# A four-layer conv and attention hybrid: the first layer's tables of batches two to four, made during batch one

## The chip, the cores and the metric

The kernel runs on one core of one Trainium2 chip. The time is device microseconds of one execution of the whole program; five runs were timed, and one more execution was taken by the hardware profiler.

## The reference, cut to what matters

The input x has 4 batches of 64 x 64 positions and 128 channels, in fp32. Four layers follow each other; each adds its result to x:

```python
x = x + _L0_conv_ref(_gn(x), ...)     # deformable attention over 9 points, 4 groups
x = x + _L1_conv_ref(_gn(x), ...)     # linear attention
t = t + _L2_attn_ref(_ln_t(t), ...);  t = t + _L2_ffn_ref(_ln_t(t), ...)   # 64 experts
t = t + _L3_attn_ref(_ln_t(t), ...);  t = t + _L3_ffn_ref(_ln_t(t), ...)   # spectral filters
```

Layer 0 works on the group-normalised image. A 1x1 product and a 3x3 depthwise convolution give q, k and v. From q come, for each position, 36 offsets (4 groups of 9 points) and a mask. At each offset position k and v are sampled with the four neighbours' bilinear weights; the nine samples of a group are then attended to by q, and the result is projected.

```python
out = gather(y0, x0) * (1 - wy_) * (1 - wx_) + gather(y0, x0 + 1) * (1 - wy_) * wx_ \
    + gather(y0 + 1, x0) * wy_ * (1 - wx_) + gather(y0 + 1, x0 + 1) * wy_ * wx_
return out * mask[:, None]
```

All batches are independent of each other in every layer.

## The kernel before, in words

**Layer 0 has two halves for each batch.** `front(b)` makes what is gathered from, and `attend` with its helpers works off the batch's 32 tiles of 128 positions.

`front(b)` is a generator of 21 steps (`STEPS`):
- 4 steps load x in eight pieces (L398), transpose them on PE (L403) into the padded image `xT` and collect statistics; `xT` is there once.
- 1 step is the group norm: `xT` is scaled in place (L413).
- 8 steps make the table of k and v. For each of 33 tiles nine shifted products over `xT` (L427) and one for the biases (L432) add up in PSUM, two tiles to a group; ACT writes them out as `kv` (L438), and SP stores each tile twice into the table in DRAM (L444). An entry of the table so holds a position's k and v for one group and the row below beside it, and one gather of 256 numbers brings all four neighbours.
- 8 steps make the image of q: nine products (L460) and one for the biases (L471) to a group of 8 rows, a copy on ACT (L477), a store into the image `qd` in DRAM (L478).

Every group of these steps takes its PSUM tile with `bank(...)` from the pool `l0mm`, which has one buffer. The same pool gives the PSUM tiles of `where_from` and `end` below, and of the spectral filters' transposes in the later layers.

**The tiles.** A batch is eight chunks of four tiles. For the next chunk, `where_from` reads q back from `qd` (L490, L494), makes the offsets on PE (L502, L512) and `where` turns them into indices and weights on DVE. `query` puts q of two tiles into PSUM (L578). `attend` issues, for each of a tile's four groups, nine indirect DMAs on POOL (L609) into one of three buffers `gt`; DVE multiplies and reduces (L618 to L628), ACT takes the exponential (L632), DVE weighs and sums (L636 to L644). `end` projects a chunk and stores it (L660 to L673).

**Two tables.** Tables `tbl` and images `qd` are there twice; batch b uses number b % 2. Their borders are set to zero at the program's start (L379 to L387), those of number 0 by ACT's DMA queue and those of number 1 by SP's.

**The order of the work.** `hybrid` writes one program in which three streams are interleaved: the tiles of batch b, the later layers of batch b - 1 (`post.run`, paced by estimated costs; `prepare`, the setup of weights, beside batch 0), and the front of batch b + 1, of which 21 steps are spread over the first 14 of the batch's 32 tiles. For the last batch only the later layers are left, with no tiles beside them. The framework then puts each engine's instructions into an order by priority (the program's order) and readiness; buffers of a pool are handed out in the program's order. From the later layers' token stage on, the exponentials (L632) and the filters' evacuations are bound to alternate (`Turns`).

The stages of the later layers that are named below: L829 to L836 load and scale the image for layer 1, L1114 multiplies by the experts' weights, L1405 and L1429 are the spectral filters, which begin about in the middle of a batch.

Of the kernel before, what the change touches and what calls it, by code (L numbers as in the profile page):

```python
# [2 lines left out]

# [5 lines left out]
F32 = mybir.dt.float32  # L9
# [7 lines left out]
P = 128  # L17
B = 4
# [4 lines left out]
IM = HW + 2  # L23
# [12 lines left out]
TENT = G * TG + 2  # L36
# [142 lines left out]
class Layer0:  # L179
    def __init__(self, tc, k, a, x1, dram, ctx):  # L180
        nc = self.nc = tc.nc
# [7 lines left out]
        self.gp = ctx.enter_context(tc.tile_pool(name="l0g", bufs=3))  # L189
        self.mm = ctx.enter_context(tc.tile_pool(name="l0mm", bufs=1, space=PSUM))  # L190
        self.qa = ctx.enter_context(tc.tile_pool(name="l0qa", bufs=2, space=PSUM))
        self.tbl = [dram.tile([TENT, P], F32, name=f"tbl{i}") for i in range(2)]
        self.qd = [dram.tile([P, IM, IM], F32, name=f"qd{i}") for i in range(2)]
        self.blk = {}


# [34 lines left out]
        with ExitStack() as pctx:  # L231
# [139 lines left out]

            zero = pr.tile([P, 2 * TX + 2], F32, name="zero")
            nc.gpsimd.memset(zero, 0.0)
            for i in range(2):
                t = self.tbl[i][0:1, :]
                eng = (nc.scalar, nc.sync)[i]
                for g in range(G):
                    for first, n in ((0, 2 * TX + 2), (65 * TX, 2 * TX)):
                        eng.dma_start(  # L379
                            bass.AP(t.tensor, t.offset + (g * TG + first) * P, [[n, P], [1, n]]),  # L380
                            zero[:, :n],
                        )
                eng.dma_start(
                    bass.AP(t.tensor, t.offset + G * TG * P, [[2, P], [1, 2]]), zero[:, :2]
                )
                for y in (0, IM - 1):
                    eng.dma_start(self.qd[i][:, y, :], zero[:, :IM])  # L387
# [4 lines left out]
    def front(self, b):  # L392

        nc, k = self.nc, self.k
        st = self.sm.tile([P, 8, 6], F32, tag="gn_st", name="gn_st")
        for c in range(8):
            xin = self.io.tile([P, 4, C], F32, tag="xin", name="xin")
            nc.sync.dma_start(  # L398
                xin, self.x[b, c * 512 : (c + 1) * 512, :].rearrange("(t p) c -> p t c", p=P)
            )  # L400
            pt = self.bank("pt")
            for t in range(4):
                nc.tensor.transpose(pt[:, t * P : (t + 1) * P], xin[:, t, :], k.ident)  # L403
            nc.scalar.copy(
                self.xT[:, 1 + 8 * c : 9 + 8 * c, 1:65], pt.rearrange("p (y x) -> p y x", x=HW)
            )
            nc.vector.bn_stats(st[:, c, :], pt)
            if c % 2:
                yield
        rs = groupnorm(nc, k, self.sm, self.mm, st)  # L410
        for c in range(8):
            part = self.xT[:, 1 + 8 * c : 9 + 8 * c, 1:65]
            nc.scalar.activation(part, part, AF.Identity, bias=rs[:, 1:2], scale=rs[:, 0:1])  # L413
        yield


        tbl = self.tbl[b % 2][0:1, :]
        ind = self.ind.rearrange("p y x -> p (y x)")
        for i0 in range(0, NK, 2):
            n = min(2, NK - i0)  # L420
            pm = self.bank("pm").rearrange("p (t o) -> p t o", t=2)
            kv = self.io.tile([P, 2, G, 64], F32, tag="kv", name="kv")
            for t in range(n):
                i = i0 + t
                for tap in range(K2):
                    at = i * P + tap // 3 * IM + tap % 3
                    nc.tensor.matmul(  # L427
                        pm[:, t, :], lhsT=self.xf[:, at : at + P], rhs=self.wd[:, tap, C:],
                        start=(t == 0 and tap == 0), stop=False,
                    )  # L430
                at = 0 if i == 0 else 5 * IM - P if i == NK - 1 else IM + i * P % IM
                nc.tensor.matmul(  # L432
                    pm[:, t, :], lhsT=ind[:, at : at + P], rhs=self.vb[:, C:],
                    start=False, stop=(t == n - 1),
                )
            for t in range(n):
                i = i0 + t
                nc.scalar.activation(  # L438
                    kv[:, t].rearrange("p g s -> p (g s)"), pm[:, t, :], AF.Identity,
                    scale=self.real[:, i : i + 1],  # L440
                )
                for slot in range(2):
                    at = (2 - slot) * TX + 2 + i * P
                    nc.sync.dma_start(  # L444
                        bass.AP(
                            tbl.tensor, tbl.offset + at * P + 64 * slot,
                            [[P, P], [TG * P, G], [1, 64]],
                        ),
                        kv[:, t],
                    )  # L450
            if i0 % 4 == 2:
                yield


        for c in range(8):
            pm = self.bank("pm")
            pv = pm.rearrange("p (y x) -> p y x", x=HW)
            for tap in range(K2):
                dy, dx = divmod(tap, 3)
                nc.tensor.matmul(  # L460
                    pv, lhsT=self.wd[:, tap, :C],
                    rhs=self.xT[:, 8 * c + dy : 8 * c + dy + 8, dx : dx + HW],
                    start=(tap == 0), stop=False,
                )
            parts = [(0, 8, 1)]
            if c == 0:
                parts = [(0, 1, 0), (1, 8, 1)]
            elif c == 7:
                parts = [(0, 7, 1), (7, 8, 4)]
            for y0, y1, e in parts:  # L470
                nc.tensor.matmul(  # L471
                    pv[:, y0:y1, :], lhsT=self.vb[:, :C],
                    rhs=self.ind[:, e : e + 1, :HW].to_broadcast([P, y1 - y0, HW]),
                    start=False, stop=(y1 == 8),
                )
            qo = self.qo[c % 2]
            nc.scalar.copy(qo[:, :, 1:65], pv)  # L477
            nc.sync.dma_start(self.qd[b % 2][:, 1 + 8 * c : 9 + 8 * c, :], qo)  # L478
            yield

    def where_from(self, b, c):

        nc, k = self.nc, self.k
        blk = self.blk[b, c] = Ctx()
        qd = self.qd[b % 2]
        q3 = self.io.tile([P, 3, 8, HW], F32, tag="q3", name="q3", bufs=1)
        for tap in range(K2):
            dy, dx = divmod(tap, 3)
            j, i = tap % 4, tap // 4
# [106 lines left out]
    def attend(self, b, c, t):  # L596
# [8 lines left out]
        for g in range(G):  # L605
            gt = self.gp.tile([P, K2, 256], F32, tag="gt", name="gt")
            for i in range(K2):
                col = g * K2 + i
                nc.gpsimd.indirect_dma_start(  # L609
                    out=gt[:, i, :], out_offset=None, in_=self.tbl[b % 2][:, :],  # L610
                    in_offset=bass.IndirectOffsetOnAxis(
                        ap=blk.idx[:, t, col : col + 1], axis=0
                    ),
                )
# [1106 lines left out]
def hybrid(tc, a, out):  # L1721
# [3 lines left out]
    with ExitStack() as ctx:  # L1725
# [13 lines left out]
        with ExitStack() as l0ctx:  # L1739
# [10 lines left out]
            for b in range(B):  # L1750
# [3 lines left out]
                for c in range(8):  # L1754
                    ahead = (b, c + 1) if c < 7 else (b + 1, 0) if b + 1 < B else None
                    l0.begin(b, c)
                    for t in range(4):
                        slot = 4 * c + t
                        if t == 0:

                            if slot == 0 and b == 0:
                                for _ in front:
                                    pass
                            if ahead:
                                l0.where_from(*ahead)
                            l0.query(b, c, 1)
                        elif t == 2 and ahead:
                            l0.query(*ahead, 0)
                        for g, _ in enumerate(l0.attend(b, c, t)):
                            turns.mark()  # L1770
                            while spent < total * (4 * slot + g + 1) / 128:
                                spent += next(behind, total)
                            if post.paced:
                                turns.took("behind")
                        if t == 0 and last:
                            l0.end(*last)
                            last = None
                        if t == 2 and ahead:
                            l0.where(*ahead)
                        if b + 1 < B:  # L1780
                            if slot == 0:
                                front = l0.front(b + 1)
                                steps = 0
                            while steps < STEPS and steps < STEPS * (slot + 1) / 14:
                                next(front)
                                steps += 1
                            if slot == 14:
                                for _ in front:
                                    pass
                    blk = l0.blk[b, c]  # L1790
                    nc.vector.tensor_add(
                        blk.xr, blk.xr, l0.bproj.unsqueeze(1).to_broadcast([P, 4, C])
# [2 lines left out]
                    if c == 7:  # L1795
                        l0.end(*last)
                        last = None
                for _ in behind:
                    pass
        post.mm = None  # L1800
        post.wide = True
# [37 lines left out]
```

## Time and profile before

| | us |
|---|---|
| median of 5 runs | 7798.72 (7791.05 to 7804.5) |
| profiled execution | 7799.04 |
| its span, first to last instruction | 7797.3 |
| first gather issued | 250.6 |
| gathers (L609) | 4608, POOL busy 4398.9 |

The four batches of tiles lie at 250 to 1699, 1699 to 3278, 3278 to 4899 and 4899 to 6497 us by their gathers; what follows to 7797 is the last batch's later layers. Front 0 runs from 13 to 329 us. The front of batch 1 runs from 342 to 861 us, that of batch 2 from 1731 to 2395, that of batch 3 from 3311 to 4039. Mean granted TensorE clock over the span: 0.823.

In lines of the profile, the engine comes after the line of the kernel; `out<-in` are the program's names of tiles; in timelines the first two numbers are start and length in us, and the bracket is the idle time of that engine before and what ended it. PE's fp32 products stand as two records each.

### The profile page before, as it was taken

The page shows a single profiled execution, that of the slowest core. Times are in us where ns is not written, and L with a number is a line of the kernel's source. Part 1 is how long each engine was busy: PE and PEld are TensorE (multiplying, and loading weights), DVE is VectorE, ACT ScalarE, POOL GpSimd, SP SyncE. Part 2 cuts the span into 40 slices and gives each one's busy share as a digit, 9 for nine tenths or more (in the row PEclk, how much of TensorE's full clock was granted, in tenths as well). Part 3 has the DMA queues.
Part 4 walks back from the last instruction along what each step waited for, and adds up shares of the span by engine and source line. Part 5 has one row for each costly group of instructions (what it writes and reads, how often), then busy time and mean ns, then how long its engine had stood idle before and what let it go on. Part 6 is the DMA issues. An engine that isn't in the chain of part 4 may idle for free.

```text
span 7797.3 us, 86706 instructions
## 1 busy us (share of the span) xinstructions
PE 5468.2 (70%) x30155; PEld 3865.5 (50%) x30155; DVE 4647.5 (60%) x7777; ACT 2256.1 (29%) x4160; POOL 4407.8 (57%) x4736
## 2 busy tenths in 40 slices
PE   7556200017887898967977999646679997577998
PEld 6343100004635676636455777322457775345776
DVE  1466666669766566688666666786766655332222
ACT  4110000003423343324233444233234433322221
POOL 0577777777773677776736777766557772000000
PEclk9778655557988999979988999766789998678999
DMA  6655444445794777666947776657667665343223
GB/s 204 192 163 137 124 114 116 118 117 150 232 281 123 189 173 170 169 173 189 281 138 199 172 173 167 176 158 243 183 174 173 165 165 164 92 149 107 72 69 83
DMA packets 1130830, 1255.00 MB, mean 161 GB/s; under 512 B 392478, under 2 KB 923161, under 8 KB 1126169
## 3 DMA queue, kind: packets, MB, share of 16 engines
q1 hardware_dynamic: 906797, 644.20, 30.6%
q0 software_dynamic: 221184, 604.27, 28.1%
q8 instruction: 239, 3.92, 0.2%
q14 instruction: 198, 1.62, 0.1%
q10 hardware_dynamic: 2412, 0.98, 0.1%
HBM read 1061.76 MB, written 187.22 MB: 160 GB/s over the span
## 4 chain that ended last, share of the span: by engine, by line
POOL 34%; PE 26%; issue 16%; DMA 11%; DVE 10%; ACT 3%; SPq 1%; DVEq 0%; ACTq 0%; POOLq 0%
POOL gt L609 34%; PE pa L1429 9%; DMA gt<-tbl,idx 6%; PE pq L1405 3%; PE pm L427 2%; DMA xin<-x 2%; DVE o L644 2%; DVE pr L618 1%; DVE s L623 1%; PE pm L460 1%; PE ph L1114 1%; DVE pv L641 1%; PE pa L1225 1%; PE pn L1235 1%; DVE ln_st L130 1%
## 5 line engine op out<-in xcount | busy, mean ns | idle before, releaser
L609 POOL DMA_INDIRECT gt<-tbl,idx x4608 | 4398.9, 955 | 2049.4 <-issue 1343.1
L1429 PE MATMUL pa<-y,m 128*128 128x256 f32 x8192 | 1937.0, 390 | 0.0
L1429 PEld LDWEIGHTS pa<-y,m 128*128 128x128 f32 x8192 | 1538.6, 193 | 370.9 <-issue 168.5
L618 DVE TENSOR_TENSOR pr<-gt,qa 128x1152 f32<-128x1152 f32 x512 | 691.4, 1350 | 961.0 <-DMA gt<-tbl,idx 945.0
L1419 ACT COPY y<-pq 128x1024 f32<-128x1024 f32 x896 | 868.7, 1014 | 1167.2 <-PE pq L1405 1165.4
L644 DVE TENSOR_REDUCE o<-pv 128x32 f32<-128x1152 f32 x512 | 1079.9, 2109 | 2.4 <-issue 1.4
L1405 PE MATMUL pq<-th,xh 32*128 32x256 f32 x8192 | 641.1, 416 | 205.5 <-ACT y L1419 154.5
L641 DVE TENSOR_TENSOR pv<-gt,qa 128x1152 f32<-128x1152 f32 x512 | 691.6, 1351 | 11.0 <-DVE eq L876 0.8
L632 ACT ACTIVATE ex<-sc,mx 128x9 f32<-128x9 f32 x512 | 156.1, 305 | 1860.5 <-DVE mx L628 1832.7
L623 DVE TENSOR_REDUCE s<-pr 128x36 f32<-128x1152 f32 x512 | 687.8, 1343 | 1.2 <-DVE qm L874 0.4
L427 PE MATMUL pm<-wd,xT 128*128 128x256 f32 x2376 | 595.6, 400 | 110.7 <-ACT kv L438 101.5
L1405 PEld LDWEIGHTS pq<-th,xh 32*128 32x128 f32 x8192 | 394.4, 191 | 395.4 <-issue 204.7
L427 PEld LDWEIGHTS pm<-wd,xT 128*128 128x128 f32 x2376 | 460.9, 200 | 222.4 <-ACT kv L438 120.3
L1416 DVE COPY y<-pq 128x1024 f32<-128x1024 f32 x128 | 156.7, 1224 | 466.1 <-ACT y L1419 466.1
L636 DVE TENSOR_TENSOR qa<-cw,ex 128x36 f32<-128x36 f32 x512 | 105.3, 206 | 546.8 <-ACT ex L632 544.5
L578 PE MATMUL qa<-sident,qt 128*128 128x128 f32 x256 | 55.0, 349 | 499.2 <-DVE pv L641 499.0
L460 PE MATMUL pm<-xT,wd 128*128 128x512 f32 x576 | 288.9, 642 | 62.8 <-ACT qo L477 50.9
L660 PE MATMUL pt<-ident,o 128*128 128x128 f32 x128 | 34.8, 365 | 381.6 <-DVE o L651 271.6
L578 PEld LDWEIGHTS qa<-sident,qt 128*128 128x128 f32 x256 | 44.4, 242 | 518.0 <-DVE pv L641 511.5
L1114 PE MATMUL ph<-w,pooled 128*1 128x512 f32 x512 | 236.1, 736 | 41.3 <-DMA w<-in_L_ffn_weight_dram 40.8
L147 ACT ACTIVATE ln<-xin,ln,ln 128x128 f32<-128x128 f32 x512 | 211.6, 483 | 131.4 <-DMA xin<-x 110.8
L660 PEld LDWEIGHTS pt<-ident,o 128*128 128x128 f32 x128 | 18.3, 169 | 401.8 <-DVE o L651 278.9
(373 smaller groups left out, 6236.0 us busy)
## 6 DMA issues: line engine op xcount, KB each, us to landing
w<-in_L_ffn_weight_dram SPq DMA_DIRECT2D x512, 256.0 KB
th<-th SPq DMA_DIRECT2D x512, 256.0 KB
gt<-tbl,idx POOLq DMA_INDIRECT x4608
xin<-x SPq DMA_DIRECT2D x256, 256.0 KB
x<-xin SPq DMA_DIRECT2D x160, 256.0 KB
tbl<-kv SPq DMA_DIRECT2D x264, 128.0 KB
th<-wx SPq DMA_DIRECT2D x32, 1024.0 KB
q<-qd SPq DMA_DIRECT2D x288, 64.0 KB
```

The lines of the kernel that those rows point to most:

```text
L147: self.nc.scalar.activation(dst, src, AF.Identity, bias=self.shift[:, i : i + 1], scale=self.rstd[:, i : i + 1])
L427: nc.tensor.matmul(pm[:, t, :], lhsT=self.xf[:, at : at + P], rhs=self.wd[:, tap, C:], start=(t == 0 and tap == 0), stop=False,)
L460: nc.tensor.matmul(pv, lhsT=self.wd[:, tap, :C], rhs=self.xT[:, 8 * c + dy : 8 * c + dy + 8, dx : dx + HW], start=(tap == 0), stop=False,)
L609: nc.gpsimd.indirect_dma_start(out=gt[:, i, :], out_offset=None, in_=self.tbl[b % 2][:, :], in_offset=bass.IndirectOffsetOnAxis(ap=blk.idx ...
L618: nc.vector.tensor_mul(pr, corners[:, :, 0:32], qa[:, q0 + 32 * g : q0 + 32 * g + 32].unsqueeze(1).to_broadcast([P, 4 * K2, 32]),)
L623: nc.vector.tensor_reduce(s4, pr, AX.X, ALU.add)
L641: nc.vector.tensor_mul(pv, corners[:, :, 32:64], aw.unsqueeze(2).to_broadcast([P, 4 * K2, 32]),)
L644: nc.vector.tensor_reduce(o[:, t, 32 * g : 32 * g + 32], pv.rearrange("p i s -> p s i"), AX.X, ALU.add)
L1114: nc.tensor.matmul(ph[32 * j : 32 * j + 1, :], lhsT=pooled[:, 16 * j + q : 16 * j + q + 1], rhs=w1s[j], start=True, stop=True,)
L1405: nc.tensor.matmul(pq[:, r // 2, r % 2, :, pair, :], lhsT=xh[rows, 2 * (q % 4) + pair, :], rhs=t[rows, 2 * (q % 2) + pair, :].rearrange("p ...
L1419: nc.scalar.copy(to, src)
L1429: nc.tensor.matmul(pa[:, h * 2 * P : (h + 1) * 2 * P].rearrange("p (g x) -> p g x", g=8), lhsT=s.m[u][:, KC * kc + i, :], rhs=yv[:, i], st ...
```

## The change

There are now four tables and four images of q, one for each batch, and all borders but number 0's are set to zero by SP's queue. The fronts of batches 1, 2 and 3 follow each other in one generator, and all of their 63 steps are spread over the first 30 tiles of batch 0; what should be left of them comes after batch 0. Beside batches 1, 2 and 3 no front is left.

```diff
-        self.tbl = [dram.tile([TENT, P], F32, name=f"tbl{i}") for i in range(2)]
-        self.qd = [dram.tile([P, IM, IM], F32, name=f"qd{i}") for i in range(2)]
+        self.tbl = [dram.tile([TENT, P], F32, name=f"tbl{i}") for i in range(B)]
+        self.qd = [dram.tile([P, IM, IM], F32, name=f"qd{i}") for i in range(B)]
...
-            for i in range(2):
+            for i in range(B):
                 t = self.tbl[i][0:1, :]
-                eng = (nc.scalar, nc.sync)[i]
+                eng = nc.sync if i else nc.scalar
...
-        tbl = self.tbl[b % 2][0:1, :]
+        tbl = self.tbl[b][0:1, :]
...
-            nc.sync.dma_start(self.qd[b % 2][:, 1 + 8 * c : 9 + 8 * c, :], qo)
+            nc.sync.dma_start(self.qd[b][:, 1 + 8 * c : 9 + 8 * c, :], qo)
...
-        qd = self.qd[b % 2]
+        qd = self.qd[b]
...
-                    out=gt[:, i, :], out_offset=None, in_=self.tbl[b % 2][:, :],
+                    out=gt[:, i, :], out_offset=None, in_=self.tbl[b][:, :],
...
-                        if b + 1 < B:
+                        if b == 0:
+
                             if slot == 0:
-                                front = l0.front(b + 1)
+                                fronts = chain.from_iterable(l0.front(i) for i in range(1, B))
                                 steps = 0
-                            while steps < STEPS and steps < STEPS * (slot + 1) / 14:
-                                next(front)
+                            while steps < (B - 1) * STEPS * (slot + 1) / 30:
+                                next(fronts, None)
                                 steps += 1
-                            if slot == 14:
-                                for _ in front:
-                                    pass
...
                 for _ in behind:
                     pass
+                for _ in fronts:
+                    pass
```

More of the change, by code (lines that the diff above doesn't have):

```diff
@@ L2 @@
 from contextlib import ExitStack, nullcontext
+from itertools import chain
 import concourse.bass as bass
```

## The prediction

> **What bounds the kernel now.** I read the page's slices first, then the costliest groups, a table of windows by batch, the same line (L1405) in each batch, and last the timelines of PE, ACT and SP.
>
> ```profile
> PE   7556200017887898967977999646679997577998
> POOL 0577777777773677776736777766557772000000
> L609 POOL DMA_INDIRECT gt<-tbl,idx x4608 | 4398.9, 955 | 2049.4 <-issue 1343.1
> ```
>
> POOL is busy at 7 tenths from slice 1 to slice 32 and idle in the last six. Each gather costs 955 ns and some 0.30 us of issue, 1.256 us together, 36 of them a tile: 45.2 us a tile, 181 us a chunk of four, 1448 us a batch of 32. The first gather starts at 250.6 us. The windows are the four batches and the tail:
>
> ```profile
> core 0: us, PE busy (x) PEld busy (x) DVE busy (x) ACT busy (x) POOL busy (x), PEclk, DMA share, GB/s
> 250.00:1699.00 1449.00, 397.41 (x1286) 255.24 (x1284) 918.76 (x1308) 104.91 (x365) 1097.52 (x1153) 0.63 0.47 131
> 1699.00:3278.00 1579.00, 1314.25 (x7396) 930.59 (x7396) 1095.20 (x1850) 577.85 (x1056) 1103.50 (x1153) 0.89 0.69 185
> 3278.00:4899.00 1621.00, 1347.62 (x7513) 950.97 (x7511) 1109.53 (x1867) 584.41 (x1067) 1100.22 (x1152) 0.89 0.70 186
> 4899.00:6497.00 1598.00, 1165.92 (x6655) 815.18 (x6653) 1094.73 (x1834) 550.83 (x1002) 1097.15 (x1152) 0.82 0.66 179
> ```
>
> Batch 0 is at the gathers' floor, PE idle for 72% of it. Batches 1 and 2 hold a front each and take 131 and 173 us more; batch 3 holds none, and takes 150 more too. So the front is not most of that excess. In these three the waits of POOL have one long entry each (92.6, 107.1, 95.3 us, on DVE pv L641): the gathers wait there until the layers of the batch before have reached their filter stage. Its first instruction, in the three batches:
>
> ```profile
> L1405 PE MATMUL pq<-th,xh x2032: 374/374/791, 2571.4 to 3274.3; 32*128 32x256 f32 x185
> L1405 PE MATMUL pq<-th,xh x2028: 374/374/791, 4192.5 to 4895.0; 32*128 32x256 f32 x185
> L1405 PE MATMUL pq<-th,xh x2016: 374/374/791, 5791.9 to 6487.3; 32*128 32x256 f32 x184
> ```
>
> It starts 872, 914 and 893 us into the batch, and the rest of the batch is 707, 707 and 705 us: what comes before L1405 decides.
>
> **Gain: no front in batches 1 and 2.** Batch 2 becomes what batch 3 is: 1621 to 1598, some -22 us (between -10 and -30, as batches of one kind may differ by some us). Batch 1 reaches layer 1's scaling (L836) 53 us in, batch 2 at 112, batch 3 at 115; from there to L1405 are 819, 803 and 778 us. So batch 1 could gain up to 819 - 778 = 41, if its layers start as early as now.
>
> **Cost: 22 more zero stores ahead of the first loads.** SP now issues one table's 11 zero stores, and the third load of x stands behind them:
>
> ```profile
> 17.31 6.60 SPq L379 DMA_DIRECT2D tbl<-zero  x8
> 24.34 0.32 SPq L383 DMA_DIRECT2D tbl<-zero  x1
> 25.35 0.79 SPq L387 DMA_DIRECT2D qd<-zero  x2
> 26.26 0.38 SPq L398 DMA_DIRECT2D xin<-in_x_dram  x1
> ```
>
> 11 issues take 26.26 - 17.31 = 8.95 us, so 22 more take 17.9. Nothing covers that: the transposes of that load start at 31.46 with "3.00 <-DMA xin", the norm follows, then PE runs the table and q without a hole to 235 us, and the first gather hangs on it. +18 us (7 if all cost 0.32 as L383's, 22 at most; no gain is possible, as the load can't come sooner). xr and the weights queued behind wait too, and nobody waits for them.
>
> **Cost: three fronts in batch 0.** Instructions to move per front: 32 transposes, 594 + 66 PE records for the table, 144 + 20 for q, on ACT 8 copies, 8 scalings and 33 + 8 evacuations (0.4 to 0.8 us each), on SP 66 table stores, 8 stores and 8 loads. ACT is busy 105 us of batch 0's 1449, SP issues them in some 0.55 us each, 45 a front; both have room. PE time is there too: front 0 took 13 to 329 us alone, 316 us, two more are 632, batch 0 has 1050 idle. DVE gets 16 bn_stats. DMA share goes from 0.47 towards the 0.70 that batches 1 and 2 carry with POOL busy for 1100 to 1104 us against 1098: 0 to 6 us, taken as 0.
>
> But each group of a front (pt, pm) takes the only buffer of pool l0mm, in program order, with the offsets (L502, L512) and outputs (L660, L666) of the tiles in the same row. And its evacuation stands in ACT's order behind an exp (L632) that waits for DVE:
>
> ```profile
> 459.38 4.15 PE L427 MATMUL pm<-wd,xT 128*128 128x256 f32 x18 [0.68 <-ACT xr L670]
> 477.51 0.59 PE L432 MATMUL pm<-vb,ind 128*128 128x256 f32 x2
> 488.79 6.13 PE L427 MATMUL pm<-wd,xT 128*128 128x256 f32 x18 [10.68 <-ACT kv L438]
> 646.76 4.32 PE L502 MATMUL pm<-q,weff 128*81 128x512 f32 x6 [2.84 <-ACT kv L438]
> ```
>
> ```profile
> 475.28 0.30 ACT L632 ACTIVATE ex<-sc,mx 128x9 f32<-128x9 f32 x1 [6.13 <-DVE mx L628]
> 487.62 0.30 ACT L632 ACTIVATE ex<-sc,mx 128x9 f32<-128x9 f32 x1 [11.95 <-DVE mx L628]
> 487.92 0.82 ACT L438 ACTIVATE kv<-pm,real 128x256 f32<-128x256 f32 x2
> ```
>
> The group that ends at 478 is evacuated at 488; PE stands for 10.68 us. Between 459.38 and 646.76 twelve groups ran, 15.6 us each, and the offsets that the program puts at tile 8 (612 us) came 35 us late: the buffer's chain, not the pace written in the loop, set that. Alone (202 to 217 us) a group takes 9.8. The next eight took 14.7 (663.65 to 781). I take 15 us. Offsets with outputs take 28 (431.85 to 459.38), loads with the norm 68 (342 to 410).
>
> Now the chain against the gathers, in us from the first gather; a chunk's offsets must be done, with 10 us of DVE behind them, at 181 x chunk. The new loop puts 9, 8, 9, 8, 8, 9, 8, 4 steps into the eight chunks (6 each before); a table step is 2 groups. The second front's table begins at 160 as now.
> - Chunk 0: 8 groups, to 280, offsets 300, ready 310; due 362.
> - Chunk 1 (from 308): 13 groups, to 503, ready 533; due 543.
> - Chunk 2 (531): 4 groups and 68, to 659; due 724.
> - Chunk 3 (687): 16 groups, to 927; due 905. With ACT free of exps the rest goes faster (6 and 10): ready 943, **38 late**.
> - Chunk 4 (941): 9 groups, to 1076; in time.
> - Chunk 5 (1104): 68 and 8 groups, to 1292, ready 1322; due 1267 + 38: 17, some 12 late.
> - Chunk 6 (1312): 13 groups, to 1507, ready 1537; due 1448 + 50: 39, some 27 late.
>
> That is 77 us of gathers standing; at 15.6 us a group the same list gives 110, at 14 it gives 35, at 13 nothing. Below nothing it can't go: batch 0 is at POOL's floor. I take +75. Then the last four q groups stand ahead of the outputs of batch 0's last chunk, which now leave 20 us after the batch's end; 40 us or so later, layer 1 of batch 0 starts later, and batch 1's gain of 41 is spent: 0.
>
> **Sum.** 18 + 75 - 22 - 0 = +71, on the profiled execution's 7799.0 us (span 7797.3; the median is 7798.7): **7870**.
>
> **Two rules of the Trainium skill.** For the change: PE is 27% busy in batch 0 and 83% in batch 1. Perfetto Trace Analysis, Optimization Strategy, says that where the most contended engine changes between regimes, interleaving them can help; by that alone the sum would be 18 - 22 - 41 = -45. Against it: the 10.68 us of idle PE above. The same page, Optimizing Tensor Performance (Matmuls), wants independent groups to rotate through PSUM banks so that evacuation overlaps the next group; l0mm has one, the change fills it denser, and by this rule the chain's 15 us stand and the sum is +71.
>
> **Rivals.**
> - **The chain keeps pace (faster).** Groups in a row already came 11.7 us apart (500.60, 512.28, 523.84). If the new order gives one group to nearly every exp, at 13 us or less, nothing waits, the last outputs leave in time, and 18 - 22 - 41 = -45, or -30 where batch 1's shorter wait leaves the layers more DVE contention: 7755 to 7770. Against: no stretch of twelve groups did better than 14.7. It decides at 13.5 us a group. 0.25.
> - **It cancels.** At 14 us: 18 + 35 - 22 - 20 = +11, 7810. 0.13.
> - **Worse.** At 15.6 us, with the late restarts after each wait counted in full: 18 + 110 - 22 + 20 = +126, 7925; the slower end of the forecast's own case.
> - **It doesn't do what it says**: the last q steps of batch 3's image run beside batch 1. In the forecast that is so, in part.
>
> The forecast's case (7815 to 7930) has 0.62. A measurement tells 0.2%, 15.6 us, from no change; so faster is 0.25, same 0.13, slower 0.62. The range runs from the faster rival's 7755 to a little past the worse one, 7935.
>
> **What would show it.** First gather near 268 us. Batch 0 longer than 1449, with POOL's waits at chunk boundaries (chunks 4, 6 and 8), the chain through L427, L438, L502; kv pairs still every 15 us. Batch 2 near 1598. If batch 0 stays at 1449 with the table groups 13 us apart or less, the forecast is wrong and the time falls near 7760; if L1405 in batch 1 starts 831 us in, the price on the last outputs was wrong.

## The result, and the profile after

The changed kernel takes 7795.2 us (median of 24 runs) against 7800.7 for the kernel before (44 runs): a ratio of 0.9994, 95% interval 0.9988 to 0.9999. That is 5.5 us, or 0.07%: no difference by the 0.2% that the prediction drew. A slowdown of 71 us was forecast. The profiled execution took 7802.2 us, its span 7800.4.

The lines of the page of after that answer to those of before:

```profile
PE   7676565665467899854667999546679987577998
POOL 0477777777674777776737777766557772000000
L610 POOL DMA_INDIRECT gt<-tbl,idx x4608 | 4401.7, 955 | 2036.1 <-issue 1338.8
```

POOL's row differs from that of before by a tenth in five slices. PE's row is what changed: slices 4 to 8 (counted from 0), which read 2, 0, 0, 0, 1 before, now read 5, 6, 5, 6, 6. The work moved, and the end did not. The windows of the four batches, cut at the first gather of each (264.9, 1716.1, 3289.0, 4894.0 and the end of the last at 6500.4):

```profile
core 0: us, PE busy (x) PEld busy (x) DVE busy (x) ACT busy (x) POOL busy (x), PEclk, DMA share, GB/s
265.00:1716.00 1451.00, 897.66 (x2964) 610.16 (x2962) 934.22 (x1332) 161.99 (x483) 1099.95 (x1152) 0.79 0.54 147
1716.00:3289.00 1573.00, 1174.89 (x6589) 814.70 (x6593) 1088.81 (x1838) 547.64 (x997) 1100.82 (x1152) 0.81 0.66 178
3289.00:4894.00 1605.00, 1172.59 (x6664) 817.25 (x6659) 1099.90 (x1853) 552.05 (x1005) 1101.43 (x1152) 0.81 0.67 180
4894.00:6500.00 1606.00, 1168.66 (x6625) 816.72 (x6629) 1095.13 (x1834) 551.39 (x1002) 1099.11 (x1152) 0.81 0.66 178
```

In batch 0 PE is busy for 500 us more (897.66 against 397.41), and the batch is 3 us longer than before. In batches 1 and 2 it is busy for 139 and 175 us less, and they are 6 and 16 us shorter. What POOL waited for in batch 0, total, times, longest:

```profile
POOL gt L610 <- DMA q<-qd: 202.4, 1, 202.4
POOL gt L610 <- DVE pv L642: 1.8, 6, 0.3
```

The 202.4 are the wait for the very first gather, which began before the window. No gather waits for `my` (L562), the last step of the sample positions: at every chunk boundary the positions were ready, at the tightest one 22 us before the gather (1429 us after the first gather, the gather at 1451). The waits that the forecast priced at 75 us are not there at all.

The start of the first gather, the four batches and the tail, in us, of the runs of this study whose chips ran alike (one profiled execution each; four runs on another chip follow below):

| kernel | first gather | batch 0 | 1 | 2 | 3 | tail |
|---|---|---|---|---|---|---|
| before | 250.6 | 1448.2 | 1579.0 | 1621.3 | 1598.5 | 1299.8 |
| after | 264.9 | 1451.2 | 1572.9 | 1605.0 | 1606.4 | 1300.0 |
| e1_old_place | 265.3 | 1448.6 | 1571.4 | 1607.7 | 1604.8 | 1295.1 |
| e2_one_front | 263.8 | 1450.1 | 1555.5 | 1598.2 | 1608.6 | 1291.3 |
| e3_dense24 | 262.9 | 1586.5 | 1556.3 | 1603.4 | 1597.8 | 1292.6 |
| e4_zeros_pool | 266.5 | 1448.9 | 1567.8 | 1600.6 | 1603.6 | 1297.1 |
| e9_before | 252.8 | 1452.9 | 1575.7 | 1611.4 | 1603.2 | 1295.4 |
| e10_borders_late | 255.7 | 1451.9 | 1574.2 | 1591.8 | 1606.9 | 1299.3 |
| e11_late_cap59 | 256.2 | 1449.5 | 1590.9 | 1592.6 | 1593.6 | 1296.4 |
| e12_dve_evac24 | 262.4 | 1583.7 | 1556.5 | 1605.9 | 1599.1 | 1301.8 |

Batch 3 holds no front in any of them and reads 1594 to 1609; the tail, 1291 to 1302. So one cell is good to some 10 to 15 us only, and the sums below go by medians where they can.

### The profile page after: what moved, and what is told of

The parts are those of the page before. It is cut to its first block, busy times and chain, and to the rows that moved or that the text cites. A ratio compares the mean times of both kernels' runs of the same rounds, so it can differ in the third digit from the quotient of the medians.

```text
span 7800.4 us, 86740 instructions
## 1 busy us (share of the span) xinstructions
PE 5666.0 (73%) x30155; PEld 3983.9 (51%) x30155; DVE 4648.3 (60%) x7777; ACT 2251.4 (29%) x4156; POOL 4410.7 (57%) x4736
## 4 chain that ended last, share of the span: by engine, by line
POOL 30%; PE 28%; issue 14%; DVE 12%; DMA 12%; ACT 4%; SPq 1%; DVEq 0%; ACTq 0%; POOLq 0%
POOL gt L610 30%; PE pa L1430 10%; DMA gt<-tbl,idx 6%; PE pq L1406 3%; DVE o L645 2%; DMA xin<-x 2%; DVE pr L619 2%; PE pm L428 2%; DMA w<-in_L_ffn_weight_dram 2%; DVE s L624 1%; DVE pv L642 1%; PE ph L1115 1%; PE pt L728 1%; PE pq L863 1%; PE pa L1226 1%
## 5 line engine op out<-in xcount | busy, mean ns | idle before, releaser
L1406 PE MATMUL pq<-th,xh 32*128 32x256 f32 x8192 | 641.5, 416 | 211.5 <-ACT y L1420 157.0
L428 PE MATMUL pm<-wd,xT 128*128 128x256 f32 x2376 | 613.4, 418 | 212.8 <-ACT kv L439 202.7
L428 PEld LDWEIGHTS pm<-wd,xT 128*128 128x128 f32 x2376 | 498.1, 212 | 314.5 <-ACT kv L439 223.4
L1406 PEld LDWEIGHTS pq<-th,xh 32*128 32x128 f32 x8192 | 394.4, 191 | 401.6 <-issue 208.9
L1115 PE MATMUL ph<-w,pooled 128*1 128x512 f32 x512 | 260.7, 837 | 72.5 <-DMA w<-in_L_ffn_weight_dram 70.5
L461 PEld LDWEIGHTS pm<-xT,wd 128*128 128x128 f32 x576 | 119.0, 212 | 255.9 <-issue 143.5
L503 PE MATMUL pm<-q,weff 128*81 128x512 f32 x192 | 125.8, 787 | 74.1 <-ACT qo L478 39.4
L863 PE MATMUL pq<-wqkv,xT 128*128 128x384 f32 x256 | 143.3, 700 | 46.9 <-DVE eq L877 44.1
```

The lines of the kernel that those rows point to most:

```text
L428: nc.tensor.matmul(pm[:, t, :], lhsT=self.xf[:, at : at + P], rhs=self.wd[:, tap, C:], start=(t == 0 and tap == 0), stop=False,)
L461: nc.tensor.matmul(pv, lhsT=self.wd[:, tap, :C], rhs=self.xT[:, 8 * c + dy : 8 * c + dy + 8, dx : dx + HW], start=(tap == 0), stop=False,)
L863: nc.tensor.matmul(pq[:, u, : 3 * C], lhsT=xT[:, (i + u) * P : (i + u + 1) * P], rhs=w.qkv1, start=True, stop=True,)
L1115: nc.tensor.matmul(ph[32 * j : 32 * j + 1, :], lhsT=pooled[:, 16 * j + q : 16 * j + q + 1], rhs=w1s[j], start=True, stop=True,)
L1406: nc.tensor.matmul(pq[:, r // 2, r % 2, :, pair, :], lhsT=xh[rows, 2 * (q % 4) + pair, :], rhs=t[rows, 2 * (q % 2) + pair, :].rearrange("p ...
```

## The experiments

The expectations name their theories (some count the batches from 1; the text here counts them from 0). In short: one says that the chain through the single buffer of `l0mm` sets the pace of the fronts and would hold up the gathers if it were filled denser, and that at 30 tiles it has time to spare; its rival, that nothing there ever binds. For the rest: the prologue's loss is the zero stores' queueing, or else something that comes with four tables.

**Four tables, the fronts in their old place** (e1). The prologue's stores alone:

```diff
-                        if b == 0:
+                        if b + 1 < B:
                             if slot == 0:
-                                fronts = chain.from_iterable(...)
+                                front = l0.front(b + 1)
                                 steps = 0
-                            while steps < (B - 1) * STEPS * (slot + 1) / 30:
-                                next(fronts, None)
+                            while steps < STEPS and steps < STEPS * (slot + 1) / 14:
+                                next(front)
```

> Four tables and their zero stores as in the changed kernel, but the fronts where they stood before (one beside each of batches 0 to 2, over 14 tiles). Theory A (the change moved three terms: +14 us ahead of the first gather, some -20 us in batches 1 and 2, nothing in batch 0): first gather near 265 us, batches near 1448, 1579, 1621, 1598 us, so 14 us (0.18%) above the kernel before, about 7813. Rival (the later batches got longer or shorter for the four tables themselves, by their place in DRAM): batch 3 near 1606 instead of 1598 here too, and the sum off by those 8 us.

Measured 7799.7 us (11 runs) against 7788.1 for before on that chip (27): 1.0014 [1.0005, 1.0023], 12 us slower. The first gather is at 265.3, as in after. So the stores cost this much whatever is done with the fronts. Batch 3 reads 1604.8 us, as the rival had it; but the kernel before reads 1603.2 in e9, so it doesn't take four tables for that. In the timeline of SP of after they are seen:

```profile
17.16 6.86 SPq L380 DMA_DIRECT2D tbl<-zero  x8
...
25.96 5.25 SPq L380 DMA_DIRECT2D tbl<-zero  x8
...
32.67 4.50 SPq L380 DMA_DIRECT2D tbl<-zero  x8
...
38.82 0.93 SPq L399 DMA_DIRECT2D xin<-in_x_dram  x2
```

Eight stores took 6.86 us the first time, then 5.25 and 4.50: the later ones are cheaper, 0.66 and 0.56 us each. The third load of x goes out at 38.82 instead of 26.26, 12.6 us later, and PE meets it in its timeline:

```profile
44.12 1.09 PE L404 MATMUL pt<-ident,xin 128*128 128x128 f32 x4 [15.90 <-DMA xin<-in_x_dram]
```

It stood 15.90 us for that load, where before it stood 3.00 at 31.46. From 12.7 us there to 14.3 at the first gather.

**One front only** (e2): what a front that isn't there at all saves in batches 1 and 2. The fronts of batches 2 and 3 are left out, and the tiles of these batches read batch 1's table and image instead of their own.

```diff
-        qd = self.qd[b]
+        qd = self.qd[min(b, 1)]
...
-                    out=gt[:, i, :], out_offset=None, in_=self.tbl[b][:, :],
+                    out=gt[:, i, :], out_offset=None, in_=self.tbl[min(b, 1)][:, :],
...
-                                fronts = chain.from_iterable(l0.front(i) for i in range(1, B))
+                                fronts = chain.from_iterable(l0.front(i) for i in range(1, 2))
...
-                            while steps < (B - 1) * STEPS * (slot + 1) / 30:
+                            while steps < STEPS * (slot + 1) / 14:
```

> The fronts of batches 3 and 4 are left out, the tiles of these two read batch 2's table and image of q; batch 2's front runs beside batch 0 over 14 tiles as before. So batches 1 and 2 hold no front, and nothing of a front is left at batch 0's end. Theory A (in the changed kernel batch 1 gained only 6 us because the last q steps run 30 us past batch 0's last gather and hold up the outputs that layer 1 waits for): L836 comes 53 us into batch 1 again instead of 66, and batch 1 takes 1560 us (13 less than the changed kernel's 1573), total near 7785. Rival (batch 1 can't gain more, because with a shorter wait its layers share DVE with the tiles): batch 1 stays at 1570 to 1575 though L836 comes 13 us sooner. The prediction's price of a front in batch 1, 41 us, would give 1538.

Measured 7777.8 us (10 runs), 0.9985 [0.9975, 0.9994]; that is 21.9 below e1 on the same chip. In the profiles batch 1 is 16 us shorter than e1's and batch 2 9.5. So two fronts, which account for some 330 us of PE's busy time (1308.56 + 1337.55 in e1's two windows, 1145.85 + 1172.99 here), cost those batches 22 us in all. No way of moving them can be expected to bring more than about that. The theory held against its rival: layer 1's scaling (L836) comes 50 us into batch 1 instead of 66, and batch 1 takes 1555.5 us instead of after's 1572.9. In e3 and e12 below, which leave nothing of the fronts for batch 1 either, it takes 1556.3 and 1556.5.

**The same fronts within 24 tiles** (e3), to make the chain bind:

```diff
-                            while steps < (B - 1) * STEPS * (slot + 1) / 30:
+                            while steps < (B - 1) * STEPS * (slot + 1) / 24:
```

> The 63 steps are spread over the first 24 tiles of batch 0 instead of 30, nothing else. Theory A (the fronts run as one chain through the only buffer of l0mm, 15.8 us a group, 40 us for loads and norm, 13 us for a tile chunk's offsets and outputs; at 30 tiles this chain is ready 37 to 45 us before the gathers need it, so it costs nothing, and the prediction only sized the 13 and the 40 too large): with 10.5 steps a chunk instead of 8.4 the offsets come late at the chunk boundaries from the third or fourth on, batch 0 grows from 1451 to 1550 to 1640 us, total 7890 to 7980. Rival B (the chain does not bind: the gathers have slack from elsewhere, or the groups close up when more of them are queued): batch 0 stays within 10 us of 1451, and batch 1 is some 13 us shorter since nothing of the fronts is left at its start: total near 7785.

Measured 7912.5 us (4 runs): 1.0162 [1.0147, 1.0178]. Batch 0 takes 1586.5 us, its tiles 15, 19, 23 and 27 (counted from 0, from first gather to first gather) between 74 and 85 us rather than 45. POOL's waits in that batch:

```profile
POOL gt L610 <- DMA q<-qd: 199.8, 1, 199.8
POOL gt L610 <- DVE my L562: 141.6, 5, 40.5
```

The second line is what the forecast looked for and after lacks: 141.6 us of gathers waiting for positions, at four chunk boundaries. One of them in the timelines of PE and POOL:

```profile
1011.39 4.15 PE L428 MATMUL pm<-wd,xT 128*128 128x256 f32 x18 [0.98 <-ACT kv L439]
...
1021.27 2.80 PE L503 MATMUL pm<-q,weff 128*81 128x512 f32 x6 [0.98 <-ACT kv L439]
```

```profile
1030.12 0.98 POOL L610 DMA_INDIRECT gt<-tbl,idx  x1 [40.54 <-DVE my L562]
```

The offsets (L503) start only when the groups ahead of them in the row have gone through the buffer; the first gather of the chunk follows 9 us later, having stood for 40.54. So the mechanism exists, and costs 138 us (1586.5 less e1's 1448.6) at 24 tiles; at 30 no gather waits for it.

**The zero stores on POOL's queue** (e4), to take them from ahead of the loads:

```diff
-                eng = nc.sync if i else nc.scalar
+                eng = nc.gpsimd if i else nc.scalar
```

> The zero stores of tables 1 to 3 are issued by POOL's queue, which has nothing else to do before the first gather, instead of SP's. Theory A (the 22 more stores stand in SP's order ahead of the third load of x, and the first gather hangs on it): first gather near 241 to 244 us instead of 265, also sooner than the 250.6 of the kernel before since its 11 are off SP too; total 20 to 24 us below the changed kernel, near 7775. Rival (the loads wait for ACT's zero stores and copies or for DMA engines, not for SP's order): first gather stays at 255 to 265, total unchanged within 8 us.

Measured 7781.3 us (11 runs): 0.9990 [0.9981, 0.9999]. That is 18 us below e1, which puts a price on the fronts' move but not on the stores: the first gather, expected early, is at 266.5. SP's stores are gone, but its other issues now come slowly:

```profile
23.82 0.38 SPq L399 DMA_DIRECT2D xin<-in_x_dram  x1
25.37 0.33 SPq L742 DMA_DIRECT2D lns<-in_L_conv_ln_scale_dram  x1
27.15 0.33 SPq L754 DMA_DIRECT2D wq<-in_L_attn_Wq_dram  x1
...
41.64 1.21 SPq L399 DMA_DIRECT2D xin<-in_x_dram  x1
```

The third load goes out at 23.82, the fourth only at 41.64: between them stand eleven small loads, 17.8 us for them where e10 below, with no store on POOL, takes 11.1 for the same eleven (20.97 to 32.08). ACT's own zero stores of table 0 took 6.20 us for six rather than 4.86 in after and 5.38 in e10, and its copy of the first transposes waits behind them until 35.07. POOL was issuing its 33 stores between 9.46 and 38.37 us. The loss changed its place and kept its size.

**The borders later** (e10): only table 0 is zeroed at the start. The other tables' borders, and the first and last row of their q images, are copied from table and image 0 by SP; in the program the copies stand where each front begins.

```diff
-            for i in range(B):
+            for i in range(1):
...
-                eng = nc.sync if i else nc.scalar
+                eng = nc.scalar
...
+    def borders(self, i):
+        t, z = self.tbl[i][0:1, :], self.tbl[0][0:1, :]
+        parts = [... the 8 borders, and the last two rows ...]
+        for at, n, m in parts:
+            self.nc.sync.dma_start(<that part of t>, <the same part of z>)
+        for y in (0, IM - 1):
+            self.nc.sync.dma_start(self.qd[i][:, y, :], self.qd[0][:, y, :])
...
     def front(self, b):
+        if b:
+            self.borders(b)
```

> The late borders again, since the chip of the run before took 57 us a tile where the others take 45. Theory A: first gather at 240 to 257 us (256.3 there), 8 to 20 us below the changed kernel's 265, batch 0 at 1450 with the borders' copies in it, total some 15 us (0.2%) below the kernel before. Rival: the copies on SP delay the offsets' loads (L490) in batch 0, which has 40 us to spare at chunk 5, and batch 0 grows by what the prologue gains.

With it ran a profile of the kernel before on the same chip:

> The kernel before, unchanged, for a profile on the chip of the three that follow. Both theories: first gather at 250.6, batches at 1448, then some 1579, 1621, 1598 us on a chip like the first; the price of the fronts in batches 1 and 2 is then read on one chip.

Measured 7779.8 us (12 runs) against 7799.0 (23): **0.9976 [0.9967, 0.9985]**, 19 us faster than before, and its interval lies below that of after, [0.9988, 0.9999] (each against before on its own chip). SP's timeline has no zero store left ahead of the third load:

```profile
20.97 0.38 SPq L416 DMA_DIRECT2D xin<-in_x_dram  x1
...
34.91 0.52 SPq L398 DMA_DIRECT2D tbl<-tbl  x1
...
43.98 0.38 SPq L416 DMA_DIRECT2D xin<-in_x_dram  x1
```

The third load goes out at 20.97, sooner than in e9 (26.71), and yet the first gather is at 255.7 (e9: 252.8). So the third load alone doesn't set it: the last of the eight loads goes out at 43.98 (e9: 41.29), with small loads of weights and the first border copies between them. Of the 33 copies, 29 were issued before the first gather, well ahead of the tiles beside which the program puts them. That the loads' late end makes the 3 us that are left is read from the trace and not tested. The windows of batches 1 and 2 (columns as above), of e10 and then of e9:

```profile
1708.00:3282.00 1574.00, 1174.72 (x6588) 815.56 (x6590) 1087.45 (x1837) 546.87 (x996) 1100.89 (x1153) 0.81 0.66 177
3282.00:4873.00 1591.00, 1158.38 (x6667) 806.51 (x6659) 1099.25 (x1853) 551.75 (x1005) 1101.56 (x1152) 0.82 0.67 181
```

```profile
1706.00:3281.00 1575.00, 1312.93 (x7412) 929.16 (x7412) 1095.97 (x1850) 578.05 (x1056) 1107.72 (x1152) 0.89 0.69 185
3281.00:4893.00 1612.00, 1342.72 (x7498) 944.51 (x7495) 1108.16 (x1867) 584.11 (x1067) 1105.24 (x1154) 0.89 0.69 187
```

Batch 1 is no shorter without the front, batch 2 is by 20 us. This is the version to keep.

**The last q groups after batch 0's last outputs** (e11): e10 with the steps held back, to let the outputs go sooner.

```diff
-                            while steps < (B - 1) * STEPS * (slot + 1) / 30:
+                            while steps < min(59, (B - 1) * STEPS * (slot + 1) / 30):
```

> Late borders, and the last four q groups of batch 3's image come after the outputs of batch 0's last chunk in the program instead of before them. Theory A (these groups hold the only buffer of l0mm, so the outputs that layer 1 waits for come late): L836 comes 50 to 54 us into batch 1 instead of 66, batch 1 takes 1555 to 1560 us, total 13 us below the run with the late borders alone. Rival (the groups cost the same in batch 1's first tiles): no difference beyond 4 us.

Measured 7803.2 us (11 runs): 1.0008 [0.9999, 1.0017], 23 us slower than e10, where 13 us faster were expected. Layer 1's scaling (L836 of before, L837 in after, L854 here) starts 77 us into batch 1, where it is 66 in after; before it was 53. The timeline of PE:

```profile
1725.90 0.48 PE L678 MATMUL pt<-ident,o 128*128 128x128 f32 x1 [1.23 <-DVE o L669]
...
1731.51 10.38 PE L478 MATMUL pm<-xT,wd 128*128 128x512 f32 x18 [0.67 <-ACT xr L688]
...
1752.17 0.38 PE L158 MATMUL gn_pm<-gn_mv,gavg 128*128 128x1 f32 x2
1756.79 9.69 PE L478 MATMUL pm<-xT,wd 128*128 128x512 f32 x18 [4.24 <-ACT qo L495]
1766.31 1.03 PE L489 MATMUL pm<-ind,vb 128*128 128x512 f32 x2
1767.53 0.35 PE L166 MATMUL gn_pv<-gn_gm,gavg 128*128 128x1 f32 x2 [0.18 <-DVE gn_gm L162]
```

The outputs (L678) now come first, but the two small products of layer 1's norm (L158, L166) stand among the q groups (L478) instead, 15 us apart. The groups have to lie somewhere on PE in this stretch, and batch 1 is 17 us longer than e10's. Batch 3 is 13 us shorter, though, and the profiled execution, at 7780.9 us the fastest of the eleven, is no slower than e10's (7781.5): it shows where the outputs went, but not where the 23 us of the median come from.

**The fronts' evacuations on DVE** (e12, at 24 tiles, borders as in after). Is it ACT's order, with a copy behind an exp, that sets a group's 15 to 17 us?

```diff
-                nc.scalar.activation(kv[:, t]..., pm[:, t, :], AF.Identity, scale=self.real[...])
+                nc.vector.tensor_scalar_mul(kv[:, t]..., pm[:, t, :], self.real[...])
...
-            nc.scalar.copy(qo[:, :, 1:65], pv)
+            nc.vector.tensor_copy(qo[:, :, 1:65], pv)
```

> Evacuation on DVE with 24 tiles again, on a chip like the first, to be set against ACT's evacuation with 24 tiles (batch 0 1586 us). Theory A' (from the slow chip, where a group took 1.4 groups of gathers as on the first: the chain goes in step with the tiles because its evacuations stand among their instructions in an engine's order, on DVE as on ACT): offsets again at 530, 758, 969, 1188 us within 5%, batch 0 near 1586, total near 7900. Theory A (the wait of ACT's exponential alone): offsets come in time, batch 0 at 1450 to 1480.

Measured 7913.3 us (2 runs): 1.0151 [1.0131, 1.0171]. Batch 0 takes 1583.7 us, e3 on ACT 1586.5, and POOL waits alike:

```profile
POOL gt L616 <- DVE my L568: 132.1, 4, 44.7
```

The offsets of the chunks start at 315, 524, 755, 963 and 1188 us from the first gather, in e3 at 305, 530, 758, 969 and 1188. So the engine that evacuates is not what sets a group's time; an evacuation that stands among the tiles' instructions in its engine's order, on DVE as on ACT, is the expectation's account, and it fits but is not shown.

**Four runs on another chip**: the late borders (e5, e10's kernel), the evacuations on DVE at 30 and 24 tiles (e6; e7, e12's kernel), and late borders with DVE (e8). There the kernel before takes 28% longer (9990.9 us, 17 runs), and so do these, so they are compared only with runs of that chip.

> Tables 1 to 3 get their zero borders when their front begins, by copies in DRAM from table 0's, on SP beside batch 0's tiles, instead of before the first loads of x; no other queue carries them in the prologue. Theory A (SP's 22 more issues ahead of the third load of x cost the 14 us; the run with the stores on POOL's queue stayed at 266 us because these stores slowed the issue of SP's and ACT's DMAs): first gather at 240 to 246 us, below the 250.6 of the kernel before as table 1's stores leave SP too, batch 0 unchanged near 1451, total 19 to 25 us (0.3%) below the changed kernel. Rival (something else in the four tables holds the first gather): first gather stays at 264 to 267.

> The fronts of batches 2 to 4 have their table groups and q groups evacuated by DVE instead of ACT (33 and 8 copies a front); the rest is the changed kernel. Theory A (a group takes 15 to 17 us in the chain because its evacuation stands behind an exponential on ACT that waits for DVE): DVE's order is no better in principle but has no such wait, so a group comes down to 11 to 13 us, the offsets of chunk 5 are made near 720 us after the first gather instead of 860, the last q group ends near 1250 instead of 1481, the last outputs of batch 0 leave in time and L836 comes 50 to 53 us into batch 1: batch 1 near 1557, total 13 to 16 us below the changed kernel. Rival (the 15 to 17 us are the planner's spacing or PE's, whoever evacuates): the same W times within 5%, the same total, or up to 20 us more where DVE's copies delay the tiles.

> Evacuation on DVE as in the run before, and the 63 steps over 24 tiles instead of 30. Theory A (with groups at 11 to 13 us the denser spread fits too): batch 0 back from 1586 us (ACT's evacuation, 24 tiles) to 1450 to 1480, total below 7810. Rival (the chain's pace does not depend on who evacuates): batch 0 again near 1586, total near 7910.

> Borders late and evacuation on DVE together, 30 tiles. Theory A: the two gains add, 20 us from the prologue and 13 to 16 from batch 1, 35 us (0.45%) below the changed kernel, first gather 240 to 246 us. Rival (DVE's copies cost the tiles what they bring): no better than the run with the late borders alone.

Measured: late borders 1.0034 [1.0015, 1.0054]; evacuation on DVE at 30 tiles 1.0091 [1.0066, 1.0117], at 24 tiles 1.0177 [1.0143, 1.0211]; late borders with DVE 1.0088 [1.0062, 1.0115]. A tile takes 56 us there rather than 45 (e5: 1789.9 us for batch 0's 32), and POOL waits in batch 0 (of e5) for its own gather buffers:

```profile
POOL gt L627 <- DVE pv L659: 306.8, 44, 15.9
```

So these runs say little of the change where POOL is the bound, and e10 and e12 repeated two of them. None gained what was expected of it, and e5's first gather came at 256.3 us instead of 240 to 246. Evacuating on DVE does cost the tiles here: batch 0 takes 1846.6 us in e8 against 1789.9 in e5. Two things they do show. The chain of e6 (evacuation on DVE) reached the offsets of the fifth boundary 1093 us after the first gather, e5 (on ACT) at 1096: again the engine makes no difference to the chain. And the stretch of sixteen groups ahead of them took 371 us in e5 and 281 in after, 6.6 and 6.2 tiles of each chip: the chain goes roughly in step with the tiles.

## Why the prediction was wrong, step by step

- **"+18" for 22 more zero stores: right in its mechanism, 4 us too large.** +14.3 at the first gather (250.6 to 264.9), +14.7 in e1. The forecast priced all 22 at 0.81 us, the mean of table 1's eleven; the later ones took less. Its clause that the first gather hangs on the third load is too narrow: e4 and e10, where that load is early, show that the loads behind it count too.
- **"+75" for three fronts in batch 0: the step that failed.** It is +3. The chain was rightly seen, and e3 shows it binding; its terms were mis-sized. When the offsets of the seven chunk boundaries start, in us from the first gather:

| due (181 x chunk) | 362 | 543 | 724 | 905 | 1086 | 1267 | 1448 |
|---|---|---|---|---|---|---|---|
| predicted | 280 | 503 | 659 | 927 | 1076 | 1292 | 1507 |
| after | 241 | 472 | 579 | 860 | 1018 | 1178 | 1414 |

 With e3's 9 us from offsets to gather, the narrowest places have 36 us (905) and 25 us (1448) to spare; in after itself, where nothing hurried DVE, the positions were ready 23 and 22 us before their gathers. The forecast had these places 38 and 27 to 39 late. Where the 93 us at the end come from: 39 in the first column, since the second front's table starts at 128 and not at 160 and its first eight groups took 14 us each; 105 in the two intervals that hold a front's loads and norm (472 to 579 and 1018 to 1178: 107 and 160 us, predicted 156 and 216); and 51 back in the other four, which took 906 instead of 855 because the groups were even slower than the 15 us. The load-and-norm stretch, in PE's timeline of after:

```profile
808.24 1.12 PE L404 MATMUL pt<-ident,xin 128*128 128x128 f32 x4 [12.31 <-ACT qo L478]
...
844.20 4.79 PE L503 MATMUL pm<-q,weff 128*81 128x512 f32 x6 [0.35 <-ACT gn_gm L167]
...
859.54 4.15 PE L428 MATMUL pm<-wd,xT 128*128 128x256 f32 x18 [0.68 <-ACT xr L671]
...
878.26 6.16 PE L428 MATMUL pm<-wd,xT 128*128 128x256 f32 x18 [9.81 <-ACT kv L439]
890.09 4.15 PE L428 MATMUL pm<-wd,xT 128*128 128x256 f32 x18 [0.49 <-ACT kv L439]
...
1125.33 4.17 PE L503 MATMUL pm<-q,weff 128*81 128x512 f32 x6 [3.04 <-ACT kv L439]
```

 The first transposes are at 808.24, the next offsets at 844.20: 36 us (37 and 35 in the other two fronts), and not the 68 that were read from 342 to 410 in the kernel before. Offsets with outputs take 844.20 to 859.54, 15 us, and 12 to 28 at the seven boundaries, 17 in the mean, not 28. What the two rows of before held beside their work:

```profile
406.03 0.59 PE L165 MATMUL gn_pv<-gn_gm,gavg 128*128 128x1 f32 x2 [20.39 <-DVE gn_gm L161]
...
449.20 0.80 PE L512 MATMUL pt<-ident,cc 81*128 81x81 f32 x4 [14.55 <-ACT cc L509]
```

 In the 68 PE stood 20.39 us for the norm's step on DVE, which came between the tiles' instructions there; in after it stood 2.36 (L166, at 843.26). In the 28 it stood 14.55 us for a copy on ACT behind an exp. Both waits were charged again wherever these terms stand in the chain, as if they were work. The groups' own price was no such case: the sixteen from 859.54 to 1125.33 take 16.6 us each, with 9.81 us of idle PE in one pair as forecast, and a denser loop made them no faster than before's 15.6. So the mechanism was right and the sizes of two terms were not: 68 for 36 and 28 for some 17.
- **"-22" for batch 2 and "0" for batch 1: the sum right, its split not.** In after the two batches gave 16 and 6 us. Three pairs put the move of the fronts, batch 0's +3 included, at about -20 by medians: after against before, -5.5 less the prologue's 14.3; e4 against e1, -18.4 less 1.2; e10 against before, -19.2 less 2.9. The 41 us that batch 1 could have gained, by the forecast, were never there: e2, with no front in it and L836 at 50 us, is 16 shorter than e1. From L836 to the filters' first product (L1405 of before, L1406 in after) it takes 799 us there, against batch 3's 778 in before, which the forecast took for the least. Part of that excess lies ahead of the experts' products (354 us in e2, where batches 2 and 3 take 340 and 350) and some behind them (283 against 277 and 279); why stays open.

 The gain itself sits in the experts' stage: its 128 products (L1114, in after L1115) take 176 and 183 us from first to last in batches 1 and 2 of before, 160 and 160 in after, and 160 in batch 3 of before, which had no front beside it.
- **The price on the last outputs was too high.** They came 31 us after the end of batch 0 instead of 20, and L836 (L837 in after) starts at 66 instead of 53: 13 us, not "40 us or so". With nothing left over (e2, e3, e12) it starts at 50, and batch 1 is 16 to 17 us shorter than in after: about that is their price. The first products of the filter stage in batch 1, by line:

```profile
L1406 PE MATMUL pq<-th,xh x2016: 374/374/792, 2580.8 to 3279.8; 32*128 32x256 f32 x184
```

 It starts 865 us into the batch, against 872 before: what starts 13 later is 7 earlier here.
- **The rivals.** "The chain keeps pace" is what happened in batch 0, but not by its own condition: it asked for 13.5 us a group or less, and the groups took 16.6. Its -41 in batch 1 was wrong too, so its 7755 to 7770 was not reached. "It cancels" gave nearly the time (7810) by terms that are not the measured ones (18 + 35 - 22 - 20): that is luck. What cancelled is +14 ahead of the first gather against about -20 for the move.
- **The two rules.** The Trainium skill's Perfetto Trace Analysis, Optimization Strategy, on interleaving regimes whose busiest engines differ, held in kind: batch 0's PE goes from 27% to 62% busy (897.66 of 1451) at a cost of 3 us. The sum by it, -45, was too good by 40, because most of PE's work in batches 1 and 2 was not what they waited for: two fronts fewer bring 22 us there (e2), and the sum counted 63. The rule of the same page's Optimizing Tensor Performance (Matmuls), that independent groups rotate through several banks, is about a true stall (9.81 us of PE above), but a stall costs only what slack doesn't cover: nothing at 30 tiles, 138 us at 24. A second buffer for `l0mm` wasn't tried.

What stays open: what in the order of a tile's row makes a group of the chain take 16 us, whichever engine evacuates.

## What to carry to other kernels

A row that is read beside a bound with time to spare holds waits as well as work (20.39 of 68 us and 14.55 of 28 here); before such durations are added up to a chain, waits inside a row should be kept apart from work, and the row looked for at more than one place. When work is moved out of a stage, ask first what the stage would gain if that work were gone altogether (here 22 us for 330 us of PE's busy time), since that caps the move. And set-up stores belong behind the first loads: of after's loss of 14 us ahead of the first gather, e10 won back all but 3.

## What the runs showed of the hardware that was not expected

- While stores were issued from POOL, other queues issued more slowly: eleven small loads on SP took 17.8 us in e4 and 11.1 in e10, and six zero stores on ACT 6.20 us against 5.38. So 33 stores on a third queue cost the start as much as on SP.
- PE's granted clock follows how busy PE is: in batch 0 from 0.63 to 0.79, in batches 1 and 2 from 0.89 to 0.81 as their fronts left. The products of L1406 keep their durations, 374/374/792 ns against 374/374/791, but others pay: the experts' products (L1114, in after L1115) take 830 and 826 ns in the mean in batches 1 and 2 of after, 613 and 617 before. Their stage got shorter even so, as said above; in batch 1 PE stood 57.8 us for the weights' loads in it, 10.5 before. Over the whole span the same 30155 PE records are busy for 5666.0 us against 5468.2, so busy time taken out of a stage is no measure of the work that left it.
- A table product that follows an idle stretch is slower: in the rows above the 18 records take 6.16 us after 9.81 us of idle PE and 4.15 after 0.49.
- One chip took 56 us a tile where the others take 45, with each gather's instruction as short (952 ns in e5, 955 in e10). In batch 0 of e5 DVE stood 502.0 us for ACT's exponentials (46.6 in e10), and ACT 556.4 us ahead of the table's evacuations, for something that the profile doesn't name. What is slower in that chip, no run separates.
